# Graph-convolution kernel: weights of layers two and three loaded from another engine's DMA queue

## The chip, the cores and the metric

The kernel runs on one core of a Trainium2 chip. The metric is the time of one execution on the device in microseconds (us). The profile comes from one further execution, recorded by the hardware profiler. Its engines are PE (TensorE: matmuls, with the weight loads as PEld), DVE (VectorE), ACT (ScalarE), POOL (GpSimd) and SP (SyncE). SP computes nothing here: it issues transfers. ACT and POOL issue transfers too, each through a queue of its own.

## The reference

Three layers of a relational graph convolution over 6250 nodes with 256 features, 100,000 edges sorted by destination and 8 edge types, followed by a residual layer norm and a graph attention layer:

```
for l in range(3):
    xr  = einsum('nd,rde->rne', x, W_rel[l])          # 8 matrices of 256 x 256
    agg = segment_sum(xr[edge_type, src], dst, N)
    x   = relu(agg + x @ W_root[l] + bias[l])
x = layernorm(x0 + x)
x = layernorm(x + attention(x, src, dst))             # 4 heads of 64
```

Layer l+1 gathers rows of x by the source of each edge. Any row can be asked for at once, so no edge of a layer can be gathered before all rows of the layer ahead are stored in DRAM.

## The kernel before

The order of the work on each engine is written out by hand: the whole of the three layers stands under `tc.manual_schedule()`, and each engine runs its instructions in program order. Waits between engines are semaphores, which the framework places from what reads and writes what. Each transfer issued by SP or ACT raises one of eight counts, taken in turn.

A layer (`layer`, L461) aggregates first and multiplies after. The edges lie in tiles of 128, and the tiles in groups of up to four. For each group i of the loop at L779:

- POOL gathers the source rows (`gather`, L493): one indirect DMA per edge tile, 128 rows of 1 KB from `table = xs[l]` (the input for the first layer, and x1 or x2 in DRAM for the second and third). There are 746 gathers in each layer. The few destinations with very many edges are handled apart (`count`, `products`). The buffers `msg` hold eight groups.
- DVE builds a one-hot matrix of type and destination (`onehot`, L475).
- PE multiplies the two (`windows`, L502, matmul at L514), and DVE adds the product into the accumulator S (`add`, L519, at L526).
- When all edges of a tile of 128 nodes are in, PE multiplies its rows by `wo` (the root weights, L578) and its part of S by `wr` (the weights of the eight types, L582). This is `dense` (L573). It needs the node's own rows, which SP loads five groups ahead (`load_rows`, L537, the DMA at L542) and PE transposes two groups ahead (`turn`, L545, transposes at L549).
- `finish` (L594) adds the bias on DVE (L596), applies relu on ACT (L599) and, in the first two layers, has SP store the 128 rows in DRAM (L600). There are 49 such stores in a layer. `clear` (L590) then zeroes the part of S on ACT (L591).

At the end of a layer the gathers run out first, then the last node tile is multiplied, finished and stored. The next layer then starts: `load_w` (L224) requests its weights, four one-hots are built, and the group loop begins with the first gathers. The weights have one buffer each for `wr` (2 MB) and `wo` (256 KB), so they can be requested only when the last matmul of the layer ahead has read the old ones.

In `load_w` four transfers are issued per layer: for each half of the features 1024 KB of `wr` (L228) and 128 KB of `wo` (L230). In the kernel before all come from ACT's queue, behind the relu of the last rows and the zeroing behind it.

Of the kernel before, what the change touches and what calls it, by code (L numbers as in the profile page):

```python
# [20 lines left out]
P = 128  # L21
# [137 lines left out]
def fast(tc, const, pl, x, xs, src, dst, edge_type, w_rel, w_root, bias, weight,  # L159
         attn_l, attn_r, out, flag):  # L160
    nc = tc.nc
    N, D = x.shape
    E = src.shape[0]
    L, R = w_rel.shape[0], w_rel.shape[1]
    H, DH = attn_l.shape
    KC = D // P
    NT, T, CH, WMAX = pl.NT, pl.T, pl.CH, pl.WMAX
    KR = KC * R

    with ExitStack() as top:  # L170
        tab = top.enter_context(tc.tile_pool(name="tab", bufs=1))
        ident = tab.tile([P, P], F32, name="ident")
        idx = tab.tile([P, CH * P], I32, name="idx")
        key = tab.tile([P, CH * P], F32, name="key")
        pos = tab.tile([1, CH * P], I32, name="pos")
        iota_p = tab.tile([P, 1], F32, name="iota_p")
        eps = tab.tile([P, 1], F32, name="eps")
        bias_b = tab.tile([P, L, D], F32, name="bias_b")
        w1x = tab.tile([P, KC, D + 2 * H], F32, name="w1x")
        altab = tab.tile([P, NT, H], F32, name="altab")  # L180
        al3 = tab.tile([P, 3, NT, H], BF16, name="al3")
        ga = tab.tile([P, NT, H], F32, name="ga")
        hif = tab.tile([P, NT], F32, name="hif")
        dt = tab.tile([P, NT], F32, name="dt")
        yT0 = tab.tile([P, KC, P], F32, name="yT0")


        A = tab.tile([P, NT, HOT * R], F32, name="A")

        psi = top.enter_context(tc.tile_pool(name="psi", bufs=1, space=PSUM))  # L190
        iota = psi.tile([P, max(R * WMAX, NT * R)], F32, name="iota")
        hk = tab.tile([P, pl.TH], F32, name="hk")
        hl = tab.tile([P, pl.TH], F32, name="hl")

        dram = top.enter_context(tc.tile_pool(name="lanes", bufs=1, space=DRAM))
        lane = dram.tile([NT * P], I32, name="lane")
        with tc.tile_pool(name="ps_p", bufs=2, space=PSUM) as ps_p:
            tables(tc, pl, ps_p, src, dst, edge_type, ident, idx, key, pos, iota, iota_p,
                   lane, hk, hl, hif, dt, flag, R, H)
        y = dram.tile([NT * P, D], F32, name="y")  # L200

        with ExitStack() as s:
            wp = s.enter_context(tc.tile_pool(name="wp", bufs=1))
            sp = s.enter_context(tc.tile_pool(name="sp", bufs=1))
            mp = s.enter_context(tc.tile_pool(name="mp", bufs=8))
            op = s.enter_context(tc.tile_pool(name="op", bufs=AHEAD + 2))
            xp = s.enter_context(tc.tile_pool(name="xp", bufs=3))
            hp = s.enter_context(tc.tile_pool(name="hp", bufs=1))
            ps_w = s.enter_context(tc.tile_pool(name="ps_w", bufs=4, space=PSUM))
            ps_d = s.enter_context(tc.tile_pool(name="ps_d", bufs=2, space=PSUM))  # L210
            ps_t = s.enter_context(tc.tile_pool(name="ps_t", bufs=1, space=PSUM))


            S = [sp.tile([P, KR, n * P + PAD], F32, name=f"S{f}") for f, n in enumerate(NS)]

            hold = {j: sp.tile([P, KR, P], F32, name=f"hold{j}") for j in sorted(pl.shared(pl.TM))}

            nc.vector.memset(eps, EPS)
            for t in S:
                nc.scalar.memzero(t)  # L220
            nc.sync.dma_start(bias_b, bias.rearrange("l d -> (l d)").partition_broadcast(P))
            fold_weights(tc, mp, w1x, weight, attn_l, attn_r)

            def load_w(l):  # L224
                wr = wp.tile([P, KC, R, D], F32, name="wr")
                wo = wp.tile([P, KC, D], F32, name="wo")
                for k in range(KC):
                    nc.scalar.dma_start(  # L228
                        wr[:, k], w_rel[l, :, k * P:(k + 1) * P, :].rearrange("r p e -> p r e"))
                    nc.scalar.dma_start(wo[:, k], w_root[l, k * P:(k + 1) * P, :])  # L230
                return wr, wo

            groups = pl.order()

            ready = {}
            for i, (f, g) in enumerate(groups):
                for j in pl.reach(g):
                    ready[f, j] = i

            with tc.manual_schedule():  # L240
                for l in range(L):
                    wr, wo = load_w(l)
                    opn = layer(
                        tc, pl, l, l == L - 1, groups, ready, S, hold, A, hk, hl, idx, key, pos,
                        iota, ident, wr, wo, bias_b, x, xs, eps, w1x, altab, y,
                        (al3, ga, hif, yT0, lane, dst, iota_p),
                        mp, op, xp, hp, ps_w, ps_d, ps_t, H)

        with tc.manual_schedule():
            attention(tc, pl, opn, A, al3, ga, hif, dt, yT0, iota, ident, eps, w1x, altab, y, out, H)  # L250
# [192 lines left out]
def fold_weights(tc, mp, w1x, weight, attn_l, attn_r):  # L443

    nc = tc.nc
    D = weight.shape[0]
    H, DH = attn_l.shape
    KC = D // P
    nc.sync.dma_start(w1x[:, :, :D], weight.rearrange("(k p) e -> p k e", p=P))
    for i, a in enumerate((attn_r, attn_l)):  # L450
        t = mp.tile([P, GT, D], F32, name="msg")
        ab, pr = t[:, 0], t[:, 1:1 + KC]
        nc.sync.dma_start(ab, a.rearrange("h d -> (h d)").partition_broadcast(P))
        nc.vector.tensor_tensor(pr, w1x[:, :, :D], ab.unsqueeze(1).to_broadcast([P, KC, D]),
                                ALU.mult)
        for k in range(KC):
            nc.vector.tensor_reduce(w1x[:, k, D + i * H:D + (i + 1) * H],
                                    pr[:, k].rearrange("p (h d) -> p h d", h=H), AX.X, ALU.add)
# [915 lines left out]
```

## Time and profile before

| what | us |
|---|---|
| median of 3 runs | 2976.59 |
| lowest and highest of them | 2976.0, 2979.49 |
| profiled execution | 2982.89 |
| its span | 2981.1 |
| PE busy with matmuls | 2671.0 (90% of the span) |
| POOL busy | 2140.4 (72%) |
| DVE busy | 1668.5 (56%) |
| ACT busy | 458.6 (15%) |

The profiled execution is one more run, and 1.8 us of it lie outside the span. TensorE's granted clock was 0.936 of full speed on average. Issuing instructions (a DMA on SP or ACT) aren't counted as busy. A gather on POOL is, and takes 0.95 us with a pause of 0.30 us before the next. Three stretches with 746 gathers each make up the layers. The first gathers of the second and third layer start at 968.0 and 1924.1 us from the start of the span.

### The profile page before, as it was taken

The page shows a single profiled execution, that of the slowest core. Times are in us where ns is not written, and L with a number is a line of the kernel's source. Part 1 is how long each engine was busy: PE and PEld are TensorE (multiplying, and loading weights), DVE is VectorE, ACT ScalarE, POOL GpSimd, SP SyncE. Part 2 cuts the span into 40 slices and gives each one's busy share as a digit, 9 for nine tenths or more (in the row PEclk, how much of TensorE's full clock was granted, in tenths as well). Part 3 has the DMA queues.
Part 4 walks back from the last instruction along what each step waited for, and adds up shares of the span by engine and source line. Part 5 has one row for each costly group of instructions (what it writes and reads, how often), then busy time and mean ns, then how long its engine had stood idle before and what let it go on. Part 6 is the DMA issues. An engine that isn't in the chain of part 4 may idle for free.

```text
span 2981.1 us, 45287 instructions
## 1 busy us (share of the span) xinstructions
PE 2671.0 (90%) x15710; PEld 2428.2 (81%) x15711; DVE 1668.5 (56%) x4094; ACT 458.6 (15%) x602; POOL 2140.4 (72%) x2254
## 2 busy tenths in 40 slices
PE   5999999999877799999988998689999999999985
PEld 4989888888776688988887887678888888888874
DVE  7645677764433455554444443256566655554778
ACT  2111111111001011111111110111111111110114
POOL 6777777777775777777777777577777777777741
PEclk9999999999988899999999997789999999998985
DMA  4444344445433444444444543344444444454534
GB/s 153 125 122 122 119 123 120 120 134 158 146 117 106 122 125 122 125 124 118 120 119 142 170 125 118 117 119 128 130 127 130 123 129 127 133 177 135 165 119 166
DMA packets 203053, 388.97 MB, mean 130 GB/s; under 512 B 42885, under 2 KB 128004, under 8 KB 202820
## 3 DMA queue, kind: packets, MB, share of 16 engines
q0 software_dynamic: 107424, 293.48, 33.6%
q1 hardware_dynamic: 87464, 85.04, 8.8%
q10 hardware_dynamic: 7932, 7.48, 0.8%
q8 instruction: 130, 2.13, 0.3%
q14 instruction: 103, 0.84, 0.1%
HBM read 360.18 MB, written 25.65 MB: 129 GB/s over the span
## 4 chain that ended last, share of the span: by engine, by line
PE 69%; POOL 10%; issue 8%; DVE 6%; DMA 5%; ACT 2%; DVEq 0%; ACTq 0%; POOLq 0%; SPq 0%
PE pw L514 31%; PE pd L582 29%; POOL msg L497 10%; PE pd L578 4%; DMA msg<-x,idx 3%; DVE S L526 3%; PE pd L686 1%; DMA msg<-in_x_dram,idx 1%; PE pt L549 1%; PE pt L630 1%; ACT xT L552 1%; PE pd L657 1%; ACT o L1053 0%; DMA wr<-in_L_gnn_W_rel_dram 0%; DVE oh L481 0%
## 5 line engine op out<-in xcount | busy, mean ns | idle before, releaser
L497 POOL DMA_INDIRECT msg<-x,idx x1492 | 1419.7, 952 | 513.9 <-issue 413.7
L514 PE MATMUL pw<-oh,msg 128*128 128x160 f32 (+22 forms) x8952 | 1305.7, 303 | 202.8 <-DMA msg<-x,idx 99.8
L514 PEld LDWEIGHTS pw<-oh,msg 128*128 128x128 f32 x8952 | 1250.9, 202 | 268.2 <-issue 127.8
L526 DVE TENSOR_TENSOR S<-S,pw 128x320 f32 (+22 forms) x2238 | 905.3, 405 | 998.1 <-PE pd L582 509.0
L582 PE MATMUL pd<-wr,S 128*128 128x256 f32 x4704 | 1108.8, 386 | 1.7 <-DVE S L526 1.4
L582 PEld LDWEIGHTS pd<-wr,S 128*128 128x128 f32 x4704 | 896.3, 194 | 118.0 <-DVE S L526 3.6
L497 POOL DMA_INDIRECT msg<-in_x_dram,idx x746 | 709.2, 951 | 236.1 <-issue 208.4
L481 DVE TENSOR_TENSOR oh<-iota,key 128x640 f32<-128x640 f32 (+23 forms) x564 | 364.2, 647 | 26.5 <-issue 14.8
L591 ACT ACTIVATE S<-S 128x2048 uint32<-128x2048 uint32 x150 | 285.0, 1900 | 0.1
L552 ACT COPY xT<-pt 128x256 f32<-128x256 f32 x195 | 72.3, 371 | 983.6 <-PE pt L549 983.5
L599 ACT ACTIVATE h<-pd 128x256 f32<-128x256 f32 x98 | 37.6, 384 | 933.5 <-DVE pd L596 752.3
L578 PE MATMUL pd<-wo,xT 128*128 128x256 f32 x588 | 170.0, 415 | 3.3 <-ACT h L599 3.3
L596 DVE TENSOR_TENSOR pd<-pd,bias_b 128x256 f32<-128x256 f32 x147 | 63.2, 430 | 172.5 <-PE pd L582 172.5
L578 PEld LDWEIGHTS pd<-wo,xT 128*128 128x128 f32 x588 | 111.2, 207 | 13.3 <-ACT h L599 3.7
L648 DVE TENSOR_SCALAR sel<-iota,hk 128x392 bf16<-128x392 f32 x138 | 80.4, 613 | 0.0
L613 ACT ACTIVATE rs<-mv,eps 128x1 f32<-128x1 f32 x49 | 14.4, 295 | 417.9 <-DVE mv L612 417.9
L686 PE MATMUL pd<-msg,A 128*128 128x256 f32 x294 | 72.5, 390 | 1.5 <-DMA msg<-x 1.5
L686 PEld LDWEIGHTS pd<-msg,A 128*128 128x128 f32 x294 | 56.7, 200 | 8.7 <-issue 1.9
L549 PE MATMUL pt<-ident,xin 128*128 128x128 f32 x294 | 57.6, 278 | 1.4 <-ACT xT L552 1.4
L630 PEld LDWEIGHTS pt<-w1x,xT 128*128 128x128 f32 x192 | 26.6, 201 | 35.2 <-ACT xT L552 35.2
L549 PEld LDWEIGHTS pt<-ident,xin 128*128 128x128 f32 x294 | 41.6, 146 | 12.9 <-ACT xT L552 2.6
L630 PE MATMUL pt<-w1x,xT 128*128 128x4 f32 x192 | 30.8, 266 | 23.5 <-ACT xT L552 23.5
(187 smaller groups left out, 640.0 us busy)
## 6 DMA issues: line engine op xcount, KB each, us to landing
msg<-x,idx POOLq DMA_INDIRECT x1492, 2.7
x<-h SPq DMA_DIRECT2D x96, 128.0 KB
xin<-x SPq DMA_DIRECT2D x96, 128.0 KB
msg<-x SPq DMA_DIRECT2D x24, 512.0 KB
msg<-in_x_dram,idx POOLq DMA_INDIRECT x746, 2.7
y<-yt SPq DMA_DIRECT2D x49, 128.0 KB
wr<-in_L_gnn_W_rel_dram ACTq DMA_DIRECT2D x6, 1024.0 KB
xin<-in_x_dram SPq DMA_DIRECT2D x48, 128.0 KB
```

What stands on the lines that cost most here:

```text
L481: nc.vector.tensor_tensor(oh[:, :len(g), :w], iota[:, :w].unsqueeze(1).to_broadcast([P, len(g), w]), key[:, g[0]:g[-1] + 1].unsqueeze(2).t ...
L497: nc.gpsimd.indirect_dma_start(out=msg[:, q, :], out_offset=None, in_=table, in_offset=bass.IndirectOffsetOnAxis(ap=idx[:, t:t + 1], axis=0))
L514: nc.tensor.matmul(pw[:, k * w:(k + 1) * w], msg[:, q, k * P:(k + 1) * P], oh[:, q, :w], start=True, stop=True)
L526: ins = nc.vector.tensor_tensor(o, o, pw.rearrange("p (a b) -> p a b", b=W), ALU.add)
L549: nc.tensor.transpose(pt[:, k * P:(k + 1) * P], t[:, k * P:(k + 1) * P], ident)
L552: nc.scalar.copy(xT.rearrange("p k n -> p (k n)"), pt[:, :D])
L578: nc.tensor.matmul(pd[:, :D], xT[:, k], wo[:, k], start=(k == 0), stop=False)
L582: i = nc.tensor.matmul(pd[:, :D], s[:, k * R + r], wr[:, k, r], start=False, stop=(k == KC - 1 and r == R - 1))
L591: i = nc.scalar.memzero(cols(f, j))
L630: nc.tensor.matmul(pt[:, :H], yT[:, k], w1x[:, k, D + H:D + 2 * H], start=(k == 0), stop=(k == KC - 1))
L648: nc.vector.tensor_scalar(oh, iota[:, :NT * R], float(512 * n), hk[:, t:t + 1], op0=ALU.add, op1=ALU.is_equal)
L686: nc.tensor.matmul(ph[:, :D], A[:, j], t[:, n], start=(n == 0), stop=(j == js[-1]))
```

## The change

The weights of the first layer are requested from ACT's queue as before, those of the second and third from SP's queue.

```diff
             def load_w(l):
+
+                q = nc.sync if l else nc.scalar
                 wr = wp.tile([P, KC, R, D], F32, name="wr")
                 wo = wp.tile([P, KC, D], F32, name="wo")
                 for k in range(KC):
-                    nc.scalar.dma_start(
+                    q.dma_start(
                         wr[:, k], w_rel[l, :, k * P:(k + 1) * P, :].rearrange("r p e -> p r e"))
-                    nc.scalar.dma_start(wo[:, k], w_root[l, k * P:(k + 1) * P, :])
+                    q.dma_start(wo[:, k], w_root[l, k * P:(k + 1) * P, :])
                 return wr, wo
```

In the built kernel the order of instructions on PE, DVE and POOL, and their waits, are those of before. At each of the two places where a layer ends, ACT has four transfers fewer and SP four more. On SP they stand behind the store of the last 128 rows (L600) and ahead of the three first loads of node rows of the new layer (L542). The eight counts are taken by the same transfers as before.

## The prediction

> **What bounds the kernel now.** I read the chain that ended last first, then the waits of POOL, then the timeline at the two places where a layer ends, since only there the change moves anything.
>
> The page's chain, shares of the span:
>
> ```profile
> PE 69%; POOL 10%; issue 8%; DVE 6%; DMA 5%; ACT 2%; DVEq 0%; ACTq 0%; POOLq 0%; SPq 0%
> ```
>
> PE carries most of it, POOL's gathers (with the "issue" pauses between them) come second. Which of the two paces a layer is seen from POOL's waits over the whole run (total us, times, longest):
>
> ```profile
> POOL msg L497 <- issue: 622.0, 2041, 0.6
> ...
> POOL msg L497 <- PE pw L514: 47.0, 110, 3.6
> POOL msg L497 <- DMA wr<-in_L_gnn_W_rel_dram: 41.1, 2, 20.7
> ```
>
> A gather starts every 1.25 us (0.95 + 0.30), and 745 steps of that are 931 us. Start to start, the second layer's stream takes 934.8 us (968.0 to 1902.8): POOL hardly ever stops in it. In the third layer the stream takes 955.8 us: there POOL stops for PE. So the second layer is paced by gathers, the third mostly by PE. Both begin with the first gather, which in both layers waits some 20 us for the layer ahead to end. Timeline at the first of these places (start, us, engine, line):
>
> ```profile
> 961.78 0.43 DVE L596 TENSOR_TENSOR pd<-pd,bias_b 128x256 f32<-128x256 f32 x1 [7.33 <-PE pd L582]
> ...
> 962.24 0.38 ACT L599 ACTIVATE h<-pd 128x256 f32<-128x256 f32 x1 [7.78 <-DVE pd L596]
> 962.25 0.38 ACTq L228 DMA_DIRECT2D wr<-in_L_gnn_W_rel_dram  x1
> 962.52 1.90 ACT L591 ACTIVATE S<-S 128x2048 uint32<-128x2048 uint32 x1
> 962.65 0.32 SPq L600 DMA_DIRECT2D x<-h  x1
> 962.67 0.59 ACTq L230 DMA_DIRECT2D wo<-in_L_gnn_W_root_dram  x1
> 963.30 0.47 ACTq L228 DMA_DIRECT2D wr<-in_L_gnn_W_rel_dram  x1
> 963.80 1.66 ACTq L230 DMA_DIRECT2D wo<-in_L_gnn_W_root_dram  x1
> 968.01 0.95 POOL L497 DMA_INDIRECT msg<-x,idx  x1 [20.69 <-DMA wr<-in_L_gnn_W_rel_dram]
> ```
>
> The weights are requested 0.40 us ahead of the last store, although they stand behind the relu and the zeroing on ACT: ACT's queue hands the computing on and goes to its transfers at once. The second place has the same picture, weights at 1918.18, store at 1918.58, gather at 1924.12.
>
> The last line names the weights as what released the gather. That is an inference, and I don't follow it. In the built kernel the first gather of a layer waits for counts of the stores; where one of the counts is also used by the weights, the value it waits for was reached earlier. In the trace's records of each count the last of the store's 16 steps comes at 967.06, POOL's wait instruction for it ends just after (it begins at 967.085), and the first weights are complete only at 967.87. So the store is what is late: 4.41 us from issue to landing, and 4.68 at the second place (1918.58 to 1923.26). The stores just before it, with the queues empty, took 1.66 us (issued 952.69) and 1.67 (1908.61). The records of packets say where the time goes. The quiet store's first packet moves 0.83 us after the issue, the last one's 2.99 us after (965.64), while packets of the weights flow from 963.30 to 970.94.
>
> [...] the store's instruction takes its usual 0.32 us, but its first packet comes 2.16 us later than that of the quiet store. [...] The trace has 144 packets of the store among the 2368 of the weights[...]. [...]
>
> **The change part by part.**
>
> *ACT loses four issues per place:* 0.38 + 0.59 + 0.47 + 1.66 = 3.1 us of its queue, from 962.25 to 965.46. ACT's next work is a copy at 993.18 that waits 28.76 us for PE. Gain there 0. If ACT were needed at once, it would be 3.1 us.
>
> *SP gains the same four*, from about 963.0 (store at 962.65 plus 0.32) to 966.2. Before it issues the first, SP waits for the last matmul (over at 961.7), and at the first place for an old count of POOL; both are past. Queued behind them are the three loads of node rows:
>
> ```profile
> 962.65 0.32 SPq L600 DMA_DIRECT2D x<-h  x1
> 976.22 1.15 SPq L542 DMA_DIRECT2D xin<-x  x3
> ```
>
> SP stood waiting for DVE until 976.2, so 10 us cover the 3.2 us. Cost 0. [...] 2304 KB of weights, which took 8.7 us from issue to last packet; begun 0.75 us later they end at about 972, or 973 with the gathers among them.
>
> *The weights land later*, by 0.75 to 2 us. The first matmul that reads them is at 1006.65, 35 us after they landed (971.3). Cost 0.
>
> *The last store lands earlier.* Bounds: as fast as the quiet one (1.66 us) or as slow as now (4.4 and 4.7). I take 1.8, for weights follow at its heels. Gain 4.41 - 1.8 = 2.6 us at the first place, 4.68 - 1.8 = 2.9 at the second. From landing to gather pass 0.95 and 0.86 us as before, so the gathers begin at about 965.4 and 1921.2.
>
> *The first gathers now meet the weights*, which before were nearly through (of the first gathers only one was slowed, to 3.56 us against 2.7). The first layer shows the price: gathers issued between 34.3 and 40.5 us beside its weights (issued at 33.76) took 5.6, 5.7, 5.3, 4.9 and 4.0 us. Then the first two would land at about 971 and 972, and PE start at 972 as it does now (972.13). That needn't cost: PE is short of work here. Its third group waits for the eighth gather, which today runs into the loads of node rows (the chain):
>
> ```profile
> 977.02 4.38 DMA msg<-x,idx
> 981.40 0.14 issue
> 981.53 1.74 PE pw L514 x4
> ```
>
> With the stream 2.6 us ahead that gather is issued at 974.4, when the weights are in and the row loads aren't yet out: it lands at about 977. From there PE is ahead as far as POOL is. Bounds for this part: a loss of the whole gain of a place, if slow gathers keep PE behind to its end, and a further gain of about 2 us per place (third group at 977 where a shift of 2.6 would give 979), which only the third layer, paced by PE, could keep. I take 0.
>
> *After the start* both streams run as before, only earlier: the second layer's because POOL paces it, the third's because PE's chain there begins with the eighth gather (1932.86, landing 4.91).
>
> Sum: -2.6 - 2.9 = -5.5 us. The profiled execution of 2982.89 would become 2977.4. It lies 6.3 us above the median of the runs shown, 2976.59; I carry the difference over: **2971.1 us**, 0.18% less. Called a change is what exceeds 0.2% here, 5.95 us, about what measurements of this kernel can tell (its three runs span 3.5 us). The forecast lies 0.5 us on the near side of that, so "faster" and "no difference" are close even where all steps hold.
>
> **Rivals.**
>
> *The gathers pay it back.* The early gathers share the engines with the weights and PE starts no earlier, or DVE's one-hots and adds hold it there. For it: the slow gathers of the first layer. Against it: PE waits 10.5 us for its first and 5.3 us for its third group. The time is then 2975, anything from 2973.5 to 2977.5.
>
> *The change doesn't do what it says.* The store isn't spared, since 1.15 MB of weights requested within 1 us of it fill the engines while it writes: it lands after 4.4 us and the time stays 2976.6. [...]
>
> *Slower: node rows stuck behind the weights.* [...] PE runs its transposes in order (L549 at 992.76). Now the loads land at about 980.5, 12 us earlier. From a landing of 990 on (the shifted transposes), that is weights through at about 986 to 989 in place of 973, PE stands and each us costs one. To eat the gain and 0.2% takes 2.6 + 3.0 us more per place, weights through only at about 993: 30 us for what took 8.7. The time at that point would be 2983. Nothing in the trace points there.
>
> **How the numbers follow.** The forecast, with 4 to 9 us of gain: 0.65 (of it 0.36 beyond 5.95 us). Gathers pay it back: 0.20. Store not spared: 0.06. Slower: 0.09, in which I count PE's clock, whose throttled stretches may fall otherwise in the third layer. Range: at the low end both stores at 1.66 us and 2 us more from the third group in each layer give 2976.6 - 5.8 - 4 = 2966.8. At the high end stand the rivals without gain, with half the spread of the runs: 2978.5. The likeliest case alone spans 2967.5 to 2972.6. Faster 0.36, same 0.54, slower 0.10.
>
> **What would show it.** SP's store at both places, then four issues of weights on SP; the store landing within 2 us; POOL's idle time before the layer's first gather at about 18 us in place of 20.7 and 20.4; the first four gathers landing after 4 to 6 us; the third group of PE 2.5 to 5 us earlier against the end of the layer ahead; the streams of gathers after it as long as before (934.8 and 955.8 us). I am wrong if the store still takes over 3 us, if the stream of a layer grows by what the start gained, or if PE waits for L549 on a load of rows.

## The result and the profile after

| what | before | after |
|---|---|---|
| median of 22 runs each, us | 2977.1 | 2970.51 |
| lowest and highest, us | 2971.55, 2986.63 | 2967.06, 2980.36 |
| profiled execution: span, us | 2981.1 | 2971.1 |

The ratio of the two is 0.9979, with a 95% interval from 0.9972 to 0.9987: 6.3 us less, between 3.9 and 8.3. The forecast was 5.5 us less, in a range that the time lies in. The interval has 0.2% inside it, so whether the change is just over or just under that bound is open. Two further measurements of the changed kernel, told below, gave less.

The chain of work that ended last, by engine, has hardly moved:

```profile
PE 69%; POOL 9%; issue 7%; DVE 7%; DMA 5%; ACT 2%; DVEq 0%; ACTq 0%; POOLq 0%
```

POOL's waits over the whole run (total us, times, longest us) show one line with a new name:

```profile
POOL msg L499 <- issue: 620.5, 2036, 0.6
POOL msg L499 <- PE pw L516: 44.5, 109, 3.5
POOL msg L499 <- DMA x<-h: 35.7, 2, 18.4
```

The two waits ahead of a layer's first gather were 41.1 us together and put down to the weights. They are 35.7 us now and put down to the store. The timeline at the end of the first layer (start, us, engine, line):

```profile
961.93 0.38 ACT L601 ACTIVATE h<-pd 128x256 f32<-128x256 f32 x1 [7.78 <-DVE pd L598]
...
962.34 0.32 SPq L602 DMA_DIRECT2D x<-h  x1
962.76 0.38 SPq L230 DMA_DIRECT2D wr<-in_L_gnn_W_rel_dram  x1
963.20 0.60 SPq L232 DMA_DIRECT2D wo<-in_L_gnn_W_root_dram  x1
963.85 0.42 SPq L230 DMA_DIRECT2D wr<-in_L_gnn_W_rel_dram  x1
964.32 1.30 SPq L232 DMA_DIRECT2D wo<-in_L_gnn_W_root_dram  x1
964.99 0.94 POOL L499 DMA_INDIRECT msg<-x,idx  x1 [17.37 <-DMA x<-h]
...
972.27 8.26 PE L516 MATMUL pw<-oh,msg 128*128 128x208 f32 x32 [10.92 <-DMA msg<-x,idx]
...
976.32 1.11 SPq L544 DMA_DIRECT2D xin<-x  x3
```

The store goes first, the weights follow 0.42 us later, and the gather starts 2.65 us after the store's issue where it took 5.36. The chain names the store and its landing time, then the first gather, which is slow now (start, us, what):

```profile
962.34 1.70 DMA x<-h
...
964.99 6.38 DMA msg<-x,idx
```

At the end of the second layer the store takes longer, and the gather starts 3.57 us after its issue (5.54 before):

```profile
1914.59 0.32 SPq L602 DMA_DIRECT2D x<-h  x1
1915.00 0.39 SPq L230 DMA_DIRECT2D wr<-in_L_gnn_W_rel_dram  x1
...
1918.16 0.95 POOL L499 DMA_INDIRECT msg<-x,idx  x1 [18.35 <-DMA x<-h]
```

**Where the 10 us between the two profiled executions come from.** I cut each trace at four events:

| stretch | before, us | after, us | difference |
|---|---|---|---|
| start to the end of the first layer's last relu | 962.63 | 962.31 | -0.32 |
| from there to the second layer's first gather | 5.38 | 2.68 | -2.70 |
| second layer, first gather to last relu | 950.54 | 949.58 | -0.96 |
| from there to the third layer's first gather | 5.57 | 3.59 | -1.98 |
| from there to the end | 1056.95 | 1052.97 | -3.98 |

The change touches the second and fourth stretch: -4.7 us. The third stretch is 950.54 us in this one trace of the kernel before and 949.2 to 950.0 in eight others on chips of the usual speed, one of them (told below) of a kernel that is slower than the one before. So the 1.0 us there isn't counted as the change's. The last stretch is another matter. In seven further traces on such chips, told of below, it is between 1045.9 and 1059.8 us. It goes with the clock that TensorE was granted in that stretch itself: 1059.8 and 1059.6 us at 0.920 and 0.922, 1053.9 and 1052.4 at 0.928, 1049.9 at 0.929, 1049.3 at 0.931, 1045.9 at 0.936. The two executions in the table had 0.920 before and 0.926 after. At 0.920 the changed kernel took 1059.8 us in another trace, longer than the kernel before here. So the 4 us aren't counted as the change's either.

### The profile page after: what moved, and what is told of

Same layout as the page of the kernel before. It is cut to its first block, busy times and chain, and to the rows that moved or that the text cites. A ratio compares the mean times of both kernels' runs of the same rounds, so it can differ in the third digit from the quotient of the medians.

```text
span 2971.1 us, 45283 instructions
## 1 busy us (share of the span) xinstructions
PE 2667.1 (90%) x15710; PEld 2424.1 (82%) x15711; DVE 1669.1 (56%) x4094; ACT 458.5 (15%) x602; POOL 2139.6 (72%) x2254
## 4 chain that ended last, share of the span: by engine, by line
PE 69%; POOL 9%; issue 7%; DVE 7%; DMA 5%; ACT 2%; DVEq 0%; ACTq 0%; POOLq 0%
PE pd L584 30%; PE pw L516 30%; POOL msg L499 9%; PE pd L580 4%; DMA msg<-x,idx 3%; DVE S L528 3%; DMA msg<-in_x_dram,idx 2%; PE pd L688 1%; PE pt L632 1%; PE pt L551 1%; ACT xT L554 1%; PE pd L659 1%; DVE st L1032 0%; DVE z L1020 0%; DVE oh L483 0%
```

## The experiments

My theory: the gain is the last store escaping the weights, so only the order of the two requests counts. Rivals: it is the queue (a single one for both, or ACT freed of four issues); and the first gathers, which now meet the weights, pay part of the gain back. In the runs the times of traces are counted from the store's issue, or from the end of a layer's last relu to the next layer's first gather ("relu to gather"). A quiet store is one with no other traffic beside it.

**The changed kernel again.** No edit.

> The changed kernel once more, as the yardstick of the three runs beside it. Both theories: 5 to 8 us under the kernel before; the last store of a layer lands within 2.8 us (before 4.4 and 4.7), POOL's idle time ahead of a layer's first gather is 17.4 to 18.4 us (before 20.7 and 20.4).

Measured: 2975.47 us against 2978.87 for the kernel before, ratio 0.9987 (0.9978 to 0.9995). That is 3.9 us less, short of the 5 us expected. The trace has what was expected: relu to gather 2.67 and 3.50 us, the store landed after 1.70 and 2.61 us.

**The weights on ACT's queue, but behind the store.** ACT waits for DVE's second one-hot before it asks for them:

```diff
     ohs = [onehot(i) for i in range(min(AHEAD, NG))]
+    if l:
+        gate = xp.tile([P, 1], F32, name="gate", bufs=1)
+        nc.scalar.copy(gate, ohs[1][:, 0, :1])
+        w = load_w(l, nc.scalar)
+    wr, wo = w
```

> The weights stay on ACT's queue, but ACT first copies one column of the second one-hot, so that it requests them at about the time SP does in the changed kernel, some 0.4 us after the last store. My theory (only the order counts: the store must be asked for before the weights): the store lands within 2.8 us, POOL waits 17.4 to 18.4 us, and the time is 4 to 7 us under the kernel before. The rival (it is the queue: one ring for store and weights, or ACT freed of four issues): the store still takes over 4 us, POOL waits over 20 us, and the time stays within 1.5 us of the kernel before.

Measured: ratio 0.9986 (0.9978 to 0.9993), 4.2 us less. The timeline:

```profile
962.78 0.32 SPq L600 DMA_DIRECT2D x<-h  x1
963.18 0.37 ACTq L228 DMA_DIRECT2D wr<-in_L_gnn_W_rel_dram  x1
...
965.44 0.94 POOL L497 DMA_INDIRECT msg<-x,idx  x1 [17.59 <-DMA x<-h]
```

The store landed after 1.72 us, and relu to gather took 2.69 and 3.46 us: the changed kernel's values, with the weights on the old queue. The weights are asked for 0.4 us behind the store instead of 0.4 us ahead of it, and that did the same as the move. The rival of the queue falls.

**The weights on SP's queue, ahead of the store.** Asked for in `finish` of the layer's last node tile:

```diff
             nc.scalar.activation(h, pd[:, :D], AF.Relu)
+            stored.append(j)
+            if len(stored) == NT:
+                nxt.append(load_w(l + 1, nc.sync))
             nc.sync.dma_start(xs[l + 1][j * P:j * P + n, :], h[:n])
```

> The weights are on SP's queue, as in the changed kernel, but ahead of the last store instead of behind it. My theory (order): SP asks for them as soon as the last matmul is over, about 0.9 us before the relu ends, and its four issues of some 3.2 us hold the store back by about 2.3 us; the store then lands behind the weights in the ring, some 3 to 7 us later than in the changed kernel. POOL waits 21 to 25 us at both places, and the time is 1 to 9 us over the kernel before. The rival (ACT freed, or one ring): 4 to 7 us under the kernel before, as the changed kernel.

Measured: 2986.08 us, ratio 1.0024 (1.0014 to 1.0034), 7.1 us more.

```profile
961.15 0.38 SPq L228 DMA_DIRECT2D wr<-in_L_gnn_W_rel_dram  x1
961.58 0.57 SPq L230 DMA_DIRECT2D wo<-in_L_gnn_W_root_dram  x1
...
964.24 0.38 SPq L606 DMA_DIRECT2D x<-h  x1
971.19 0.94 POOL L500 DMA_INDIRECT msg<-x,idx  x1 [23.86 <-DMA x<-h]
```

SP's own issues hold the store back from 962.0 (end of the relu) to 964.24, and it then lands after 6.2 us, with 2304 KB of weights asked for ahead of it on its own queue (1.70 us in the changed kernel, where they stand behind it). Relu to gather: 9.16 and 9.38 us, together 7.6 more than before. Same queue, same work off ACT, opposite order, opposite sign.

**No weights for layers two and three.**

```diff
-                    wr, wo = load_w(l)
+                    wr, wo = load_w(l) if l == 0 else (wr, wo)
```

> Leaves out the loading of the weights of layers two and three; both are computed with those of the first. My theory (the slow first gathers of the changed kernel cost nothing, since PE is short of work there): the first gathers land after 2.7 us and PE's first matmul comes 3 us earlier than in the changed kernel, but the time is within 1.5 us of it, 5 to 8 us under the kernel before. The rival (the gathers pay part of the gain back): 9 us or more under the kernel before.

Measured: 2975.47 us, the same median as the changed kernel beside it; ratio to before 0.9992 (0.9985 to 1.0000). As expected it is no faster than the changed kernel. The expected gain of 5 us or more over the kernel before was too much, as it was for the changed kernel in this set. The gathers are quick here, and PE starts 4.1 us after the first one, 7.3 in the changed kernel:

```profile
966.03 0.94 POOL L497 DMA_INDIRECT msg<-x,idx  x1 [17.60 <-DMA x<-h]
...
970.14 4.81 PE L514 MATMUL pw<-oh,msg 128*128 128x208 f32 x16 [7.74 <-DMA msg<-x,idx]
```

Yet the second layer, from first gather to last relu, takes 949.95 us here, and 949.58, 949.95 and 949.84 in three traces of the changed kernel. There the slow first gathers cost nothing. In the third layer, from the last relu ahead of it to the end of its second finished node tile, 86.3 us pass in the kernel before, 85.1, 83.4 and 85.3 in three traces of the changed kernel, and 85.4 here. The line of that tile before (the relu ended at 1918.55):

```profile
2004.38 0.42 DVE L607 SCALAR_TENSOR_TENSOR h<-pd,xres 128x256 f32<-128x256 f32 x1
```

and in the first trace after (1914.57):

```profile
1999.23 0.42 DVE L609 SCALAR_TENSOR_TENSOR h<-pd,xres 128x256 f32<-128x256 f32 x1
```

So quick first gathers bring nothing there either. For the rest of the third layer only the times of the runs speak, and they exclude no more than some 2 us.

These figures show something else. Of the 2 us by which the third layer's first gather comes earlier, two of the three traces of the changed kernel have only 1.0 and 1.2 us left at the second tile. The records of the granted clock fit: in the kernel before and in these two, TensorE has half its clock from about 64 to 70.5 us after the relu. PE is idle for some 5 us around its start and goes on at 66.3 us in the kernel before, at 64.1 and 64.6 in the changed one, and so does more of its work at half clock. In the third trace the half clock ends at 67.2 us, and 2.8 us are left. That this is the cause is argued, with a single trace of the kernel before.

**How much ahead of the store does the harm?** Three kernels leave a part of the weights on ACT's queue, 0.4 us ahead of the store, and send the rest behind it on SP's. The edit in the body of `load_w`, here for 512 KB, with `types` for a range of edge types of `wr` and `root` for `wo`:

```diff
+                q = nc.sync if l else nc.scalar
+                types(nc.scalar, 0, 0, R // 2)
+                types(q, 0, R // 2, R)
+                root(q, 0)
+                types(q, 1, 0, R)
+                root(q, 1)
```

> Of the four transfers of weights of layers two and three only one of wo (128 KB) stays on ACT's queue, 0.4 us ahead of the last store; the other three follow the store on SP's queue. My theory ([...] the store's delay goes with the bytes ahead of it, at the some 400 KB per us of the weights): 128 KB take 0.3 us, less than the head start, and the store's first packet moves 0.8 to 1.1 us after its issue. Rival (any transfer on the other queue holds the store up by about 2 us, whatever its size): first packet after 2.5 us or more, as in the kernel before.

> As the run with 128 KB ahead of the store, but with half of the first transfer of wr (four of the eight types, 512 KB) on ACT's queue ahead of the store and the rest behind it on SP's. My theory: 512 KB take 1.3 us, 0.9 beyond the head start, and the store's first packet moves 1.5 to 2.0 us after its issue. Rival (size doesn't matter): 2.5 us or more, or 0.8.

> As the run with 512 KB, but with the whole first transfer of wr (1024 KB) on ACT's queue ahead of the store, and only the other three behind it on SP's. My theory: the first transfer alone makes the delay of the kernel before; first packet 2.7 to 3.2 us after the issue, store landed after 4 to 4.7 us. Rival (the three further transfers on ACT's queue matter too): under 2.3 us.

These three fell on a chip on which every kernel, the one before too, took over 3600 us. The end of a layer is hardly different there: quiet stores land after 1.66 to 1.70 us as elsewhere, and the kernel before, traced on another such chip, has 5.44 and 5.65 us from relu to gather and a first packet of the store after 3.06 and 3.13 us. So only these stretches are read. The 512 KB gave 2.9 to 3.0 us in place of the 1.5 to 2.0 of my theory. It had counted on 400 KB per us from the start (in the kernel before 92 to 108 packets of weights start in each quarter of a microsecond from 4 to 8 us after the first store's issue), but by 1.75 us after the store's issue only 57 and 53 packets of the 512 KB had started; then some 90 follow in each quarter of a microsecond. The 1024 KB gave no more than the 512 KB, and that a delay by all bytes ahead can't give. 256 KB were added on a chip of the usual speed:

> As the run with 512 KB of weights ahead of the store on ACT's queue, but with 256 KB (two of the eight types). The three sizes before gave a first packet of the store 1.1, 3.0 and 3.1 us after its issue (128, 512 and 1024 KB), which my theory that the delay goes with all bytes ahead doesn't give. Theory now: [...] the store waits for the bytes ahead of it or for about 500 KB, whichever is less. 256 KB are then through at about 1.9 us: first packet 1.6 to 2.2 us after the issue. Rival (a switch of queues costs a fixed 2 us as soon as the transfer ahead is longer than the head start): 2.8 to 3.1 us.

| ahead of the store | first packet of the store, us after its issue (both places) | packets of weights started before it, of those asked for | store landed, us | relu to gather, us |
|---|---|---|---|---|
| nothing (changed kernel) | 0.82, 0.83 | 0 | 1.70, 2.70 | 2.68, 3.59 |
| 128 KB | 1.12, 0.99 | 100, 87 of 144 | 2.15, 2.63 | 3.13, 3.52 |
| 256 KB | 1.86, 1.78 | 203, 179 of 272 | 2.85, 3.26 | 3.74, 4.12 |
| 512 KB | 2.96, 2.91 | 489, 460 of 528 | 3.93, 4.76 | 4.82, 5.61 |
| 1024 KB | 3.06, 3.06 | 516, 529 of 1040 | 4.45, 4.75 | 5.42, 5.64 |
| all, on ACT (kernel before) | 2.99, 3.11 | 537, 551 of 2368 | 4.41, 4.68 | 5.38, 5.57 |

The packets are counted in the trace's records by queue. A packet here moves 1 KB, and 16 more of 4 bytes close each transfer. Up to 512 KB most of what was asked for first has started when the store's first packet moves (60 to 93% in the table), and the rest starts within 0.6 us. With 1024 KB and more, the store's first packet comes when some 500 have started (516 to 551), and from then on packets of both queues start: with 1024 KB ahead the half microsecond from 3.0 us on holds 133 packets of weights beside 56 of the store, the next one 118 beside 81. The store is then also drawn out from 0.5 to 1.1 us, which the 512 KB, nearly through by then, don't do (0.4 and 0.5 us). From the store's first packet to its first closing one pass 0.68 us or more, 0.34 where nothing is ahead. What sets the some 500 packets wasn't shown. The new theory foretold the 256 KB; the rival of a fixed 2 us falls.

**The weights still later: behind two loads of node rows.** Asked for in the group loop, some 10 us after the store:

```diff
             held[j] = load_rows(j)
+            asked.append(j)
+        if w is None and len(asked) == 2:
+            w = load_w(l, nc.sync)
```

> All four transfers of weights on SP's queue, but behind the first two loads of node rows of the new layer instead of ahead of them, some 10 us after the last store. The store lands as in the changed kernel. The first gathers land after 2.7 us in place of 5 to 6, PE's first matmul comes about 3 us earlier, and gathers about eight to fourteen are slowed to 4 to 6 us instead. My theory (what the gathers lose to the weights isn't on the path): 2 to 7 us under the kernel before, as the changed kernel. Rival (the slowed first gathers hold the layer up): 7 us or more under it. A third way: the weights come too late, PE waits in front of its first multiplication with wo, and the time is over that of the changed kernel.

This first measurement fell on the slow chip: ratio 0.9979 (0.9961 to 0.9997). I don't build on it, since on that chip POOL waits 328 us for PE where it waits 44.5 to 47.4 in four traces from others. The second measurement, beside the changed kernel:

> The changed kernel again, beside a second look at the weights behind the row loads. 0.998 to 0.999 of the kernel before, as in its two earlier measurements.

> The weights behind the first two loads of node rows once more, since the first time fell on a chip on which every kernel, the one before too, took over 3600 us. On a chip of the usual speed my theory gives the time of the changed kernel within 2 us: the first gathers are no longer slowed, but they weren't on the path. The rival (they hold the layer up) gives 3 us or more under the changed kernel. If the weights come too late, PE waits ahead of its first multiplication with wo, and it is over the changed kernel.

Measured: changed kernel 2974.79 us, ratio 0.9993 (0.9984 to 1.0002), a smaller gain than the 0.998 to 0.999 expected; weights behind the rows 2976.41 us, ratio 0.9996 (0.9987 to 1.0006). The first six gathers land after 2.7 to 2.8 us and PE starts about 3 us earlier against the relu, but now the gathers from the seventh on meet the weights and take 5 to 6 us, and PE stands before its third group:

```profile
968.82 4.82 PE L514 MATMUL pw<-oh,msg 128*128 128x208 f32 x16 [7.72 <-DMA msg<-x,idx]
...
973.68 0.38 SPq L228 DMA_DIRECT2D wr<-in_L_gnn_W_rel_dram  x1
...
979.91 6.98 PE L514 MATMUL pw<-oh,msg 128*128 128x208 f32 x32 [6.27 <-DMA msg<-x,idx]
```

The second layer takes 949.54 us. PE doesn't wait for the late weights: they have landed at 986.5 and are first read at 1003.4. Nothing is gained over the changed kernel, nor clearly lost. No run here clearly beats the changed kernel.

**The kernel before once more**, for its trace:

> The kernel before once more, for its trace alone: one trace of it is too few to say what of the 10 us between the two profiled executions is the change. My theory: from the end of the last relu to the next layer's first gather 5.2 to 5.7 us at both places as in the first trace (the changed kernel: 2.7 and 3.5 to 3.7), the second layer between these 949 to 951 us, while the stretch from the third layer's first gather to the end falls anywhere between 1046 and 1060 us with the granted clock. Rival (the change shortens the third layer itself by some 4 us): that stretch is 1055 us or more also at a granted clock of 0.938 or above.

It fell on a slow chip too (3607.12 us, clock 0.876). The two stretches at the ends of the layers are confirmed, 5.44 and 5.65 us. What it was to say of the third layer it can't say.

All runs against the traces, the two stretches from relu to gather beside the measured ratio:

| kernel | relu to gather, sum against before, us | measured, us (95%) |
|---|---|---|
| changed kernel, three measurements | -4.7, -4.8, -4.6 | -6.3 (-8.3 to -3.9), -3.9 (-6.6 to -1.5), -2.1 (-4.8 to +0.6) |
| on ACT behind the store | -4.8 | -4.2 (-6.6 to -2.1) |
| on SP ahead of the store | +7.6 | +7.1 (+4.2 to +10.1) |
| no weights | -4.4 | -2.4 (-4.5 to 0.0) |
| behind the row loads | -4.7 | -1.2 (-3.9 to +1.8) |

Every interval but the last holds the sum of its traces. For the weights behind the row loads the interval ends 0.8 us short of it. Its trace shows nothing given back: the second layer is no longer than the others', the third layer's second tile ends 85.1 us after the relu, as in the changed kernel, and the last stretch of 1052.4 us is in line with the others at its clock of 0.928. Of seven such intervals one can miss by chance; whether something is lost later in the third layer isn't settled. The three measurements of the changed kernel, weighted by their intervals, give 4.4 us less, 0.15%.

## Why the prediction was right

**The store is what is late.** Right. The line that named the weights as the releaser was an inference, and the records of the counts were the better witness. In the changed kernel the profile itself names the store, and the gather starts at 964.99, while the first weights land only at 967.84.

**The last store lands earlier.** No trace had shown, when I made the forecast, that weights behind it on its own queue leave it alone. Its first packet now moves 0.82 and 0.83 us after its issue, where 2.99 and 3.11 us passed with the weights ahead of it. The forecast was a landing after 1.8 us at both places. The first has 1.70 us in three traces. The second has 2.70, 2.61 and 2.83: the term was 0.9 us too small there, and the gain of that place 2.0 us in place of 2.9. The weights aren't the cause, for with none at all the second store took 2.87 us. Of its 16 steps, 15 come by 1.68 us as at the first place, and only the last is late. Beside it one packet of 8 KB moves on a queue of the kind "instruction". In all traces, of the last two stores of the first and of the second layer that have nothing else ahead of them, 14 have such a packet within 1.6 us of their issue and land after 2.20 to 2.87 us, with the fifteenth step at 1.66 to 1.68; 28 have none and land after 1.65 to 1.72. In the 11 of the 14 whose packets can be told from the weights', nine packets of the store, a sixteenth of its 144, are late, and the first of them starts within 0.01 us of the end of the 8 KB packet. That one of the 16 DMA engines that the page counts was held up is my estimate, from these nine of 144: the records don't name the engine.

**ACT's and SP's issues cost nothing.** Right: SP's four end at 965.6, its next work starts at 976.3, and the run with the weights on ACT shows that freeing ACT brings nothing. **Later weights** cost nothing: landed at 972.3, first read after 1005.

**The first gathers meet the weights.** Nearly right in size, too: 6.4, 5.9, 5.2 and 4.0 us against the forecast 4 to 6, PE's first matmul at 972.27 against 972, the eighth gather landed at 976.7 against 977. PE runs into its third group without a stop, 14.6 us after the relu in place of 18.9.

**After the start** the streams of gathers are no longer than before: 933.9 and 952.0 us, against 934.8 and 955.8. But the forecast let the third layer keep its whole start, and the traces show part of it lost by the second node tile in two of three, as told with the run without weights. For that the forecast had no term.

**The sum.** 5.5 us forecast; the traces have 4.7 at the first gathers, the runs 6.3 in the first measurement and 4.4 over all three. The mechanism holds, and the term of the second store is what was mis-sized. That the first measurement reads higher than the traces is within its interval. So it is partly luck that the time of 2970.51 us came within 0.6 us of the forecast 2971.1: the two later measurements gave a smaller gain.

**The rivals.** "The gathers pay it back" falls for the second layer (949.6 to 949.95 us with and without weights) and for the start of the third (second tile 83.4 to 85.3 us after the relu with weights, 85.4 without), and stays open for the rest of the third below 2 us. "The store isn't spared" falls. "Node rows stuck behind the weights" falls: the row loads land after 4.4 us as before (4.2).

**What I had too small** is the spread: I took 3.5 us from three runs, and 22 runs of the kernel before span 15 us. In the traces it comes from the last stretch, which holds the third layer, paced by PE, and whose length goes with the granted clock (1059.8 us at 0.920, 1045.9 at 0.936). A difference of two profiled executions is then no measure of the change. Here it was 10 us for a change of 4.7.

## What to carry to other kernels

Where a small store releases the next stage, look at what else is asked for in the microsecond around it. A bulk load requested 0.4 us earlier on another queue cost that store 2.7 us at the first place, and the same load 0.4 us later cost it nothing. Here the order in time counted, not the queue: moving the load and delaying it gave the same (2.68 and 2.69 us from relu to gather, 5.38 before). Behind the store on its own queue is the simplest way to fix the order, and ahead of it on its own queue was the worst of those tried (9.16 us from relu to gather).

## What the runs showed of the hardware

- A 128 KB store asked for 0.4 us behind a load on another queue had its first packet 1.1, 1.9, 3.0 and 3.1 us after its issue with 128, 256, 512 and 1024 KB in that load, and 0.8 us with nothing ahead. By then 60 to 93% of the packets of the three smaller loads had started, and 516 to 551 packets of 1024 KB and of 2304 KB; after that packets of both queues started (133 of the load beside 56 of the store in half a microsecond).
- With a packet of 8 KB on a queue of the kind "instruction" within 1.6 us of its issue, a 128 KB store landed after 2.20 to 2.87 us in 14 cases, with 15 of its 16 steps there by 1.68; without one it landed after 1.65 to 1.72 us in 28. In the 11 cases of the 14 whose packets can be told apart, the store's last nine packets start when the 8 KB packet ends.
- ACT's queue issued transfers that stand behind two ACT instructions before these were done: the kernel before requested the weights at 962.25, and ahead of them in ACT's order the relu ran from 962.24 to 962.62 and the zeroing from 962.52 to 964.42.
- Two of the chips ran the kernel before in 3607 to 3627 us instead of 2977, at a granted clock of 0.87 to 0.88 instead of 0.94. In three traces from there POOL waits 317 to 338 us for PE, in four from elsewhere 44.5 to 47.4. The cause wasn't sought.
